# Two inner sums of the first Winograd tree on VectorE instead of GpSimd

## The chip, the core and the metric

The program runs on one core of a Trainium2 chip. The core has five instruction queues that matter here: TensorE (PE in the profile, with its weight loads as PEld), VectorE (DVE), ScalarE (ACT), GpSimd (POOL) and SyncE (SP), which issues most of the transfers. The metric is the device time of one execution in microseconds (us). All times below are in us unless marked ns.

## What is computed

With x of shape (1024, 512), 64 weight matrices W_e of 512 x 512, a linear layer and a bias, all in float32:

```
out_lin = x @ lin_w.T + lin_b
xv = jnp.einsum('bf,efm->bem', x, weight)
zp = jnp.einsum('bf,efm->bem', jnp.square(x), jnp.square(weight))
interaction = 0.5 * jnp.sum(jnp.square(xv) - zp, axis=1)
return out_lin + interaction
```

The second einsum needs no product per e: since it is summed over e, the kernel sums the squared weights over e first (`w2_sum`) and multiplies x squared with that once. The first one is the work: 64 products of 1024 x 512 by 512 x 512, squared and summed.

## The kernel before, in words

The model columns and the 64 values of e are laid out so that a *group* is one weight block of 512 features by 2048 columns. A group is multiplied by Winograd's form of Strassen's scheme, with seven products in place of eight, applied twice. At the outer level the weight block has four quarters, W11, W12, W21 and W22 (tiles `w11`, `w12`, `w21`, `w22a` or `w22b`), two sums `T1` and `T2`, and seven outer products, numbered 1 to 7; each is one call of `tree(s, g, i, order)`, with `RHS` naming the tile it reads. At the inner level a tree has again seven products, which I call p1 to p7, on the quarters b11, b12, b21, b22 of its tile and on four *inner sums*: t1 = b12 - b11, t2 = b22 - t1, t3 = b22 - b12, t4 = b21 - t2. p5 reads t1, p6 reads t2, p7 reads t3 and p4 reads t4; p1, p2 and p3 read quarters as they were loaded. The four sums go into four rings of two buffers each, `t1_0`, `t1_1` and so on; the first tree (`s` = 0) takes those with `_0`, the next one those with `_1`.

The X side (`x_all`, parts `X1` to `X7`, each with seven slots) is built once at the start from the quarters of x, by ACT copies and DVE sums, and stays in SBUF. In the same opening stretch the kernel computes the linear layer with four large products of its own (`lin_product`, line 461, the operands `oa`, `ob` and the DVE sums `w22b`) and, later and in between the first trees, a joint tree of three small products (`lin_tree`, line 821; its own inner sums are the POOL operations that write `ob`).

A tree's products go into three PSUM banks: `b3` takes p5 and then p3 on top of it, `b1` takes p1 and then p2, and a ring of two, `b2`, takes a copy of p1 on which p6, p7 and p4 are added one after another. Between them ACT copies banks to SBUF (`p5`, `p53`, `b2`), and DVE adds them (`oa1` after p6, `oa3` after p7). So the next product into a bank waits for the ACT copy or the DVE sum that reads it.

What runs where, and in which order on each queue, is settled by a planner in the file itself (`class Plan`). Every operation is added with its cost on the engines that may run it, its reads and its writes; PE's order is given by a key. `order()` works out the latest start of everything backwards from PE's sequence and then simulates the engines forward, each taking the ready operation with the earliest latest start. An operation added with `both=True` is one on DVE with two inputs in SBUF; for these the planner lengthens either DVE's or POOL's work when they overlap. The emitted queues are in order: an instruction that waits holds everything behind it.

Lines that the change and the prediction touch: `two_input` (306) makes a sum or difference for one engine, and line 312 is its instruction, whatever the engine; `tree` (646) with the loop over the four sums (650 to 657), `product` (663, matmuls at line 668) and the order of products at the end (726 to 743); `PLACE_0`, the order of the very first tree's products, p5, p1, p3, p6 first; `x_sum` (409), the X-side sums, recorded at 312 or 417; `outer_sum` (608), which for the first group makes `T1` and `T2` on DVE in halves.

Of the kernel before, what the change touches and what calls it, by code (L numbers as in the profile page):

```python
# [27 lines left out]
PE, DVE, ACT, POOL, SP = "PE", "DVE", "ACT", "POOL", "SP"  # L28
# [170 lines left out]
def kernel(  # L199
# [61 lines left out]
    buf = {}  # L261
# [39 lines left out]
    plan = Plan()  # L301
# [4 lines left out]
    def two_input(engine, o, a, b, sub, size=1024):  # L306

        costs = {DVE: 0.08 + 1.06 * size / 1024, POOL: 0.14 + 2.19 * size / 1024}

        def emit(e):  # L310
            f = engines[e].tensor_sub if sub else engines[e].tensor_add
            f(o, a, b)  # L312

        return {engine: costs[engine]}, emit

    def whole(o, a, b, psum=False):

        costs, emit = two_input(DVE if psum else POOL, buf[o], buf[a], buf[b], False)
        plan.add(costs, emit, (a, b), (o,))

    def act(o, i, func, reads, writes, cost=1.04):
        def emit(_):
            if func is None:
                nc.scalar.copy(o, i)  # L324
            elif func == "negative":
                nc.scalar.mul(o, i, -1.0)
            else:
                nc.scalar.activation(o, i, func)  # L328

        plan.add({ACT: cost}, emit, reads, writes)  # L330
# [262 lines left out]
    def w(g, q):  # L593
        return q + "ab"[g % 2] if q == "w22" else q
# [37 lines left out]
    def finish(g, i, n, pos):  # L632

        row, col = {2: (0, 0), 3: (0, 1), 4: (1, 0), 5: (1, 1)}[i]
        q, cc = divmod(pos, 2)
        b, m = (row * 2 + q) * G, (col * 2 + cc) * MI
        act(buf[n], buf[n], AF.Square, (n,), (n,), 1.07)
        reduce(buf[acc_name[g]][:, b:b + G, m:m + MI], buf[n], (n,), ((acc_name[g], i, pos),))
# [7 lines left out]
    def tree(s, g, i, order):  # L646
        r = w(g, RHS[i])
        b11, b21, b12, b22 = (buf[r][:, c, k, :] for c in range(NCB) for k in range(KH))
        t = {k: t_ring[k]() for k in range(1, 5)}
        for k, a, b, reads in (  # L650
            (1, b12, b11, (r,)),
            (2, b22, buf[t[1]], (r, t[1])),
            (3, b22, b12, (r,)),
            (4, b21, buf[t[2]], (r, t[2])),
        ):
            costs, emit = two_input(POOL, buf[t[k]], a, b, True, 512)
            plan.add(costs, emit, reads, (t[k],))
        rhs = {
            1: (b11, r), 2: (b21, r), 3: (b22, r), 4: (buf[t[4]], t[4]),
            5: (buf[t[1]], t[1]), 6: (buf[t[2]], t[2]), 7: (buf[t[3]], t[3]),  # L660
        }

        def product(p, b, first):
            op, name = rhs[p]

            def emit(_):
                for j in range(G):
                    nc.tensor.matmul(  # L668
                        buf[b][:, j, :], buf[f"X{i}"][:, SLOT[p], ts(j, P)], op,
                        start=first, stop=True, skip_group_check=True,  # L670
                    )

            plan.add({PE: PAIR}, emit, (name, f"{'Y' if p == 7 else 'X'}{i}", b), (b,),
                     key=7 * s + (PLACE if s else PLACE_0)[p])

        def copy(o, b):
            act(buf[o], buf[b], None, (b,), (o,))

        def target(pos):
            if i == 2 and order.index(2) < order.index(6):  # L680
                return c_ring()
            return f"{TARGET[i]}{pos}"

        def early(pos):

            return pos == 3 and i in ADDEND_FROM and (
                order.index(i) - order.index(ADDEND_FROM[i]) > 1
            )

        def outer_psum(b, pos):  # L690

            if i == 1:
                copy(f"oa{pos}", b)
            elif i == 5:
                o = c_ring()
                whole(o, f"oa{pos}", b, psum=True)
                whole(f"ob{pos}", f"ob{pos}", b, psum=True)
                finish(g, i, o, pos)
            else:
                o = target(pos)  # L700
                whole(o, b, f"{ADDEND[i]}{pos}", psum=True)
                if i in (2, 4, 3):
                    finish(g, i, o, pos)

        def outer_sbuf(b, p, pos):

            if i == 1:
                whole(f"oa{pos}", b, p, psum=True)
            elif i == 5:
                o = c_ring()  # L710
                whole(p, b, p, psum=True)
                whole(o, f"oa{pos}", p)
                whole(f"ob{pos}", f"ob{pos}", p)
                finish(g, i, o, pos)
            else:
                a, o = f"{ADDEND[i]}{pos}", target(pos)
                if early(pos):
                    whole(o, b, p, psum=True)
                else:
                    z = p if o == a else o  # L720
                    whole(z, b, p, psum=True)
                    whole(o, z, a)
                if i in (2, 4, 3):
                    finish(g, i, o, pos)

        b2, p5, p53 = b2_ring(), p5_ring(), p53_ring()
        product(5, "b3", True)
        if early(3):
            whole(p5, "b3", f"{ADDEND[i]}3", psum=True)
        else:  # L730
            copy(p5, "b3")
        product(3, "b3", False)
        copy(p53, "b3")
        product(1, "b1", True)
        copy(b2, "b1")
        product(6, b2, False)
        outer_sbuf(b2, p53, 1)
        product(2, "b1", False)
        outer_psum("b1", 0)
        product(7, b2, False)  # L740
        outer_sbuf(b2, p5, 3)
        product(4, b2, False)
        outer_psum(b2, 2)

    def turn(g, tiles, half=True):

        row = tuple((acc_name[g], i, pos) for i, pos in acc_parts if (i in (2, 3)) + 2 * (i in (4, 5)) & tiles)
        b = {1: slice(0, NB // 2), 2: slice(NB // 2, NB), 3: slice(0, NB)}[tiles]
        a, t = buf[acc_name[g]][:, b, :], buf["turned"][:, b, :]
        size = (b.stop - b.start) / NB  # L750
        names = tuple(("turned", h) for h in range(2) if tiles & 1 << h)
        if half:
            plan.add({ACT: 0.2 + 0.25 * size}, lambda _: nc.scalar.mul(a, a, 0.5), row, row)
        plan.add(
            {DVE: 0.1 + 0.27 * size},
            lambda _: nc.vector.transpose(
                t.rearrange("p n m -> p (n m)"), a.rearrange("p n m -> p (n m)")
            ),
            row, names,
        )  # L760
        return b, names
# [141 lines left out]
    def group(g, before={}):  # L903
        acc_name[g] = acc_ring()
        for q in range(4):
            load(g, q)
        outer_sum(g, 1)
        outer_sum(g, 2)
        w_squares(g, "w12")
        order = ORDER if g else ORDER_0  # L910
        for idx, i in enumerate(order):
            if i == 1:
                w_squares(g, "w11")
            if i == 2:
                w_squares(g, "w21")
            if i == 7:
                outer_sum(g, 3)
            if i == 4:
                outer_sum(g, 4)
            if i == (5 if g < NG - 1 else 2):  # L920
                w_squares(g, "w22")
            if idx == 1 and 0 < g < 8:
                x_squares((1, 2, 4, 5, 6, 7, 3)[g - 1])
            if idx in before:
                before[idx]()
            tree(7 * g + (g > 0) + idx + sum(idx >= b for b in before), g, i, order)

    for g in range(NG - 1):
        group(g, {} if g else {2: lin_tree})
        b, names = turn(g, 3)  # L930
# [237 lines left out]
    for h in (1, 0):  # L1168
        b, names = turn(last, 1 + h, h == 1)
# [57 lines left out]
```

## Time and profile before

| | us |
|---|---|
| three timed runs | 1402.46, 1402.54, 1408.55 (median 1402.54) |
| the profiled execution | 1407.72 |
| its span, first to last instruction | 1405.9 |
| PE busy | 1397.0 (99%) |
| DVE busy | 1092.5 (78%) |
| POOL busy | 1056.2 (75%) |
| ACT busy | 714.8 (51%) |
| mean granted TensorE clock | 0.998 |

A profile is one execution. Its lines name the engine, the program line and the operation as `out<-in` with the buffer numbers left out, so `t<-w` is an inner sum of a loaded quarter. In the timeline the first two columns are the start from the beginning of the span and the length; what stands in brackets is the idle time of that engine before the instruction and what ended it. A product of a tree is two matmuls of 128x512 in float32, and each shows as two records: four records are one product. The waits table gives total, number and longest wait. In the table of stretches each engine has its busy time and its count of instructions, and PEclk is the clock that TensorE was granted.

### The profile page before, as it was taken

Reading aid. Unit: us, or ns where it says so; the run is one execution under the profiler, and the core shown is the slowest. Engines: PE = TensorE matmul, PEld = TensorE weight load, DVE = VectorE, ACT = ScalarE, POOL = GpSimd, SP = SyncE. Lnnn points to the kernel's source line nnn. Section 1 sums busy time; section 2 is a strip of 40 time slices with the busy share of each in tenths; the row PEclk is TensorE's granted clock in tenths of the full one; section 3 lists DMA queues with packets and bytes.
Section 4 is the critical chain, followed back from the end, with each engine's and each line's share of the span. In section 5 each row is a group of like instructions: output and inputs, shape, how many; then the busy total and the mean of one; then the engine's idle time right before and its main releaser. Section 6 shows DMA issues by size and latency. Waiting matters only on the chain.

```text
span 1405.9 us, 10715 instructions
## 1 busy us (share of the span) xinstructions
PE 1397.0 (99%) x3314; PEld 631.8 (45%) x3314; DVE 1092.5 (78%) x985; ACT 714.8 (51%) x756; POOL 1056.2 (75%) x752
## 2 busy tenths in 40 slices
PE   8999999999999999999999999999999999999998
PEld 4544444444444444444444444444444444444454
DVE  4898696877969778596877959678696877959676
ACT  4546364554736456374544636455373544636444
POOL 5697786867778686786868778686786958678994
PEclk9999999999999999999999999999999999999999
DMA  7397473836739285482826638184572827538363
GB/s 269 75 205 195 119 199 86 222 111 162 216 116 217 97 195 183 120 213 77 236 65 170 162 90 214 37 195 131 123 180 77 228 57 178 155 96 207 101 164 113
DMA packets 55816, 212.90 MB, mean 151 GB/s; under 512 B 21521, under 2 KB 23057, under 8 KB 33873
## 3 DMA queue, kind: packets, MB, share of 16 engines
q0 software_dynamic: 13136, 84.81, 31.2%
q1 hardware_dynamic: 40352, 125.12, 25.5%
q10 hardware_dynamic: 2272, 2.30, 0.5%
q8 instruction: 27, 0.44, 0.1%
q14 instruction: 29, 0.23, 0.1%
HBM read 180.75 MB, written 14.02 MB: 139 GB/s over the span
## 4 chain that ended last, share of the span: by engine, by line
PE 98%; DMA 1%; DVE 0%; POOL 0%; SPq 0%; ACTq 0%; issue 0%; DVEq 0%
PE b L668 96%; PE b L821 1%; PE b L1140 1%; DMA w<-weight 1%; DMA ob<-lin_wT 0%; POOL t L312 0%; DVE x_all L312 0%; SPq L354 0%; DVE c L312 0%; ACTq L361 0%; DVE w_sum L335 0%; DVE T L1119 0%; DVEq L1223 0%; DVE T L1152 0%; DVE ob L860 0%
## 5 line engine op out<-in xcount | busy, mean ns | idle before, releaser
L668 PE MATMUL b<-t,x_all 128*128 128x512 f32 x1792 | 807.9, 594 | 3.4 <-POOL t L312 3.4
L668 PEld LDWEIGHTS b<-t,x_all 128*128 128x128 f32 x1792 | 341.4, 191 | 428.9 <-issue 418.7
L668 PE MATMUL b<-w,x_all 128*128 128x512 f32 x768 | 358.2, 593 | 0.0
L312 POOL TENSOR_TENSOR t<-w 128x512 f32<-128x512 f32 x128 | 174.5, 1364 | 145.6 <-PE b L668 77.1
L324 ACT COPY p<-b 128x1024 f32<-128x1024 f32 x165 | 165.5, 1003 | 183.2 <-PE b L668 178.4
L668 PEld LDWEIGHTS b<-w,x_all 128*128 128x128 f32 x768 | 146.3, 191 | 183.7 <-issue 182.7
L312 POOL TENSOR_TENSOR t<-w,t 128x512 f32<-128x512 f32 x128 | 171.7, 1342 | 56.9 <-PE b L668 56.8
L328 ACT ACTIVATE oa<-oa 128x1024 f32<-128x1024 f32 x124 | 129.6, 1057 | 148.0 <-DVE oa L312 148.0
L324 ACT COPY b<-b 128x1024 f32<-128x1024 f32 (+1 forms) x114 | 113.5, 996 | 136.0 <-PE b L668 132.4
L668 PE MATMUL b<-T,x_all 128*128 128x512 f32 x384 | 180.3, 593 | 0.0
L335 DVE TENSOR_REDUCE acc<-oa 128x16 f32<-128x1024 f32 x124 | 148.9, 1212 | 36.7 <-ACT oa L328 36.7
L312 DVE TENSOR_TENSOR oa<-b,p 128x1024 f32<-128x1024 f32 x95 | 115.8, 1219 | 49.1 <-PE b L668 49.1
L335 DVE TENSOR_REDUCE w_sum<-wsq 128x16 f32<-128x1024 f32 x128 | 153.8, 1209 | 0.2 <-ACT wsq L328 0.2
L328 ACT ACTIVATE c<-c 128x1024 f32<-128x1024 f32 x77 | 79.6, 1055 | 125.9 <-DVE c L312 84.3
L312 POOL TENSOR_TENSOR t<-T 128x512 f32<-128x512 f32 x64 | 87.3, 1364 | 52.3 <-issue 31.0
L668 PEld LDWEIGHTS b<-T,x_all 128*128 128x128 f32 x384 | 73.1, 190 | 90.8 <-issue 88.6
L312 DVE TENSOR_TENSOR p<-b,p 128x1024 f32<-128x1024 f32 x79 | 96.5, 1221 | 20.9 <-PE b L668 16.8
L312 DVE TENSOR_TENSOR ob<-b,p 128x1024 f32<-128x1024 f32 x48 | 58.7, 1222 | 64.8 <-PE b L668 64.7
L328 ACT ACTIVATE wsq<-w 128x1024 f32<-128x1024 f32 x96 | 98.1, 1053 | 5.6 <-DMA w<-weight 3.0
L312 POOL TENSOR_TENSOR t<-T,t 128x512 f32<-128x512 f32 x64 | 81.8, 1279 | 21.1 <-PE b L668 21.0
L312 POOL TENSOR_TENSOR c<-oa,p 128x1024 f32<-128x1024 f32 x32 | 84.7, 2648 | 0.0
L312 DVE TENSOR_TENSOR oa<-b,oa 128x1024 f32<-128x1024 f32 x62 | 75.7, 1220 | 9.5 <-PE b L668 9.5
(114 smaller groups left out, 1411.0 us busy)
## 6 DMA issues: line engine op xcount, KB each, us to landing
w<-weight SPq DMA_DIRECT2D x48, 1024.0 KB, 5.3
T<-weight POOLq DMA_DIRECT2D x45, 1024.0 KB, 8.9
T<-weight SPq DMA_DIRECT2D x30, 1024.0 KB, 7.3
w<-weight POOLq DMA_DIRECT2D x16, 1024.0 KB, 11.0
w<-T POOLq DMA_DIRECT2D x16, 1024.0 KB, 6.9
w22a<-weight SPq DMA_DIRECT2D x8, 1024.0 KB, 10.6
w22b<-weight SPq DMA_DIRECT2D x8, 1024.0 KB, 10.6
c<-xT SPq DMA_DIRECT2D x9, 512.0 KB, 6.2
```

Source lines behind the costliest of these rows:

```text
L312: f(o, a, b)
L324: nc.scalar.copy(o, i)
L328: nc.scalar.activation(o, i, func)
L335: lambda _: nc.vector.tensor_reduce(o, i.rearrange("p a (m e) -> p a m e", e=E), axis=AX.X, op=ALU.add),
L668: nc.tensor.matmul(buf[b][:, j, :], buf[f"X{i}"][:, SLOT[p], ts(j, P)], op, start=first, stop=True, skip_group_check=True,)
L821: nc.tensor.matmul(buf[b][:, u, lo:lo + Q], op[z], buf[f"X{x}"][:, SLOT[p], :], start=first and not lo, stop=True, skip_group_check=True,)
L1140: nc.tensor.matmul(o, ap[:, k, ts(u, P)], in_rows(o, buf[raw[i]][:, k, lo:hi]), start=first and k == 0, stop=k == 1, skip_group_check=True,)
```

## The change

In `tree`, the first two inner sums t1 and t2 of the tree with `s` = 0, which is the first tree of the first group and reads W11, are added for DVE instead of POOL, with `both=True`; t3 and t4 of that tree, and all four sums of every other tree, stay on POOL.

```diff
             (3, b22, b12, (r,)),
             (4, b21, buf[t[2]], (r, t[2])),
         ):
-            costs, emit = two_input(POOL, buf[t[k]], a, b, True, 512)
-            plan.add(costs, emit, reads, (t[k],))
+            engine = POOL if s or k > 2 else DVE
+            costs, emit = two_input(engine, buf[t[k]], a, b, True, 512)
+            plan.add(costs, emit, reads, (t[k],), both=engine == DVE)
```

The planner then emits other queues on two engines, in the opening stretch only. PE, ACT and SP keep their orders. DVE's queue, with the line numbers of the kernel before, changes from the fourteenth instruction on:

```
before                               after
x_all<-x_all,oa   (L417, for X6)     x_all<-x_all,oa   (L417, for X6)
x_all<-oa,oa      (X7)               t1
x_all<-x_all,oa   (L417, X3)         x_all<-x_all,oa   (L417, X3)
x_all 128x2x256                      t2
x_all 128x256                        x_all<-oa,oa      (X7)
x_all 128x2x256                      x_all 128x256
x_all 128x256                        oa1<-b2,p53       (after p6)
x_all 128x2x256                      x_all 128x2x256
oa1<-b2,p53       (after p6)         x_all 128x256
x_all 128x256                        x_all 128x2x256
T1, first half                       x_all 128x256
oa3<-b2,p5        (after p7)         x_all 128x2x256
                                     T1, first half
                                     oa3<-b2,p5        (after p7)
```

On POOL, with "next" for the sums of the second tree and `ob` for those of the linear joint tree:

```
before: t1, t3, t2, next t1, ob, ob, t4, next t2, next t3, next t4, ob x6, w12<-weight
after:  t3, ob, ob, next t1, next t3, next t2, t4, next t4, ob x6, w12<-weight
```

## The prediction

> **What bounds the kernel now.** I read the chain of waits first: 98% of the span is PE, and after the opening it is one unbroken piece of matmuls.
>
> ```profile
> 57 pieces in order of time: start us, us, what
> ...
> 8.92 7.38 DMA w<-weight
> 16.30 0.07 issue
> 16.38 5.68 POOL t L312
> 22.05 0.04 issue
> 22.10 17.18 PE b L668 x36
> ...
> 66.40 1292.65 PE b L668 x3012
> ```
>
> So the span is the opening, up to where the first tree's first product starts (22.10), and then PE's work. An edit can only help where PE waits, and the table of PE's waits has four entries:
>
> ```profile
> PE b L668 <- POOL t L312: 3.4, 1, 3.4
> PE b L387 <- PEq L1216: 0.8, 1, 0.8
> PE b L821 <- DVE c L860: 0.6, 1, 0.6
> PE b L461 <- DVE w22b L312: 0.2, 1, 0.2
> ```
>
> The largest is the wait of p5 for t1, the first of the two sums that the change moves. PE's timeline and the table of stretches show that it costs more than its length:
>
> ```profile
> 15.09 3.60 PE L461 MATMUL b<-x_all,w22b 128*128 128x512 f32 x8
> 22.10 3.44 PE L668 MATMUL b<-t,x_all 128*128 128x512 f32 x4 [3.41 <-POOL t L312]
> 25.38 3.60 PE L668 MATMUL b<-w,x_all 128*128 128x512 f32 x8
> ```
>
> ```profile
> 19.00:22.00 3.00, 0.00 (x0) 0.00 (x0) 1.92 (x5) 0.99 (x2) 3.00 (x1) 0.94 1.01 369
> 23.00:24.00 1.00, 1.00 (x3) 0.37 (x2) 0.00 (x0) 0.00 (x0) 1.00 (x2) 0.50 1.02 397
> 26.00:28.00 2.00, 2.00 (x6) 0.81 (x5) 0.00 (x0) 1.24 (x2) 2.00 (x4) 1.00 0.76 293
> ```
>
> PE has nothing from 18.69 (22.10 less 3.41) to 22.10, and then p5, four records, takes 3.44 where the next eight take some 3.43: the granted clock is 0.50 right after the gap and 1.00 later. Why t1 is late stands in the timelines of POOL and DVE:
>
> ```profile
> 16.38 5.67 POOL L312 TENSOR_TENSOR t<-w 128x512 f32<-128x512 f32 x1 [15.93 <-DMA w<-weight]
> 22.01 1.26 POOL L312 TENSOR_TENSOR t<-w 128x512 f32<-128x512 f32 x1
> ```
>
> ```profile
> 17.23 1.22 DVE L417 SCALAR_TENSOR_TENSOR x_all<-x_all,oa 128x1024 f32<-128x1024 f32 x1
> 18.36 2.56 DVE L312 TENSOR_TENSOR x_all<-x_all 128x512 f32<-128x512 f32 x5
> 30.80 1.23 DVE L312 TENSOR_TENSOR oa<-b,p 128x1024 f32<-128x1024 f32 x1 [9.88 <-PE b L668]
> ```
>
> The same 128x512 sum takes 1.26 once DVE is idle, and 5.67 while DVE runs X-side sums back to back until 20.92 (18.36 plus 2.56). POOL ends 1.13 after that, nearly one undisturbed sum later. I read it as POOL shut out until DVE stops.
>
> **What the change removes and adds.** Removed from POOL: t1 (5.67 as it stood) and t2 (1.26). Added to DVE: two sums of 128x512 with both inputs in SBUF. DVE does this size in 0.69 (its sums into w22b at 9.14 and 11.75), so 1.38 in all. t1 now comes directly behind the X6 sum, which ran from 14.96 to 16.18, and must wait for w11, seen by POOL at 16.38: done at 16.38 + 0.69 = 17.07. The trace shows no DVE sum and POOL sum released by one transfer, so I bound it. Below, DVE is not hindered: 17.07. Above, POOL's t3 goes first and DVE waits for one sum: 16.38 + 1.26 + 0.69 = 18.33. I take the lower, as the DVE rows at 17.23 and 18.36 kept their usual lengths with POOL waiting. Either way t1 is there before PE has finished the linear products at 18.69, so p5 follows them without a gap.
>
> The gain at that place: 3.41 of waiting, and 3.44 - 1.72 = 1.72 of half clock, for 1.72 is a product at full clock (half of 3.43). Sum 5.13.
>
> A rule speaks against counting the second term. The Trainium skill, page "TensorE: Matmul & The Clock Gate", section "Part 1: The HAM clock gate", says that the clock falls after an idle window of about 3.4 us which runs freely, whatever the kernel does; the gap here is about as long as that window, so it may or may not fall in another execution. By the rule the sum would be 3.4 in an execution where it doesn't fall, by the row 5.1.
>
> **Whether the next waits swallow it.** With p5 at 18.69, a product each 1.72: p1 20.41, p3 22.13, p6 23.85, the next tree's p5 25.57, and everything behind 5.13 earlier than now. One by one:
>
> - p1 needs bank b1, read by ACT until 18.73 + 1.26 = 19.99. Cover 0.4. ACT's copies follow PE as they do now.
> - p6 needs t2: t1 at 17.07, the X3 sum 1.22, t2 0.69, so 18.98. Cover 4.9; with a POOL sum ahead of each still 2.4.
> - The next tree's p5 needs its t1 from POOL, now behind t3 and two `ob` sums. DVE's run ends at 18.98 + 1.22 (X7) + 0.42 = 20.62; POOL's t3 1.13 later, 21.75; the `ob` sums 0.72 and 0.45, and the sum 1.26: 24.2. Cover 1.4. If the 5.67 was a slow first instruction and not DVE, t3 ends at 22.05 and the sum at 24.5. Cover 1.1.
> - In order, DVE now holds five X sums behind oa1, which waits for p6 (25.57). They ran before, in the 9.88 of idle time. New: oa1 25.7 to 26.9, the five (0.69 three times, 0.42 twice) 2.91, T1's half 1.22, so 31.1. Who waits: oa3, due at 37.59 - 5.13 = 32.46, and PE's first joint product, which needs X3, X6 and X7, at 39.11 - 5.13 = 33.98. Cover 1.4. From below nothing is lost. From above, POOL is at work just then and each DVE sum can meet one: t4 and the next t4 (1.27 each), then `ob` of 0.72, 0.45, 0.72 and so on, in sum some 4.7. Then DVE is 4.7 - 1.4 = 3.3 late, p4 loses about 1.7 of it (oa3 done at 32.46 + 3.3 + 1.23 = 37.0, p4 due at 40.41 - 5.13 = 35.28), and at most 3.3 is lost by 60.11, where PE already waits 0.62 for DVE. The nearest row is DVE's stay at 16.09 to 20.92, where its queue never paused for a waiting POOL; I take nothing lost.
> - Behind POOL's `ob` sums stands its transfer onto w12 (issued at 40.58 after a wait of 4.41): two sums fewer are ahead of it, and its releaser moves with PE. The loads on SP from 58.04 on wait for buffers that PE frees; they move along. The loads before that are issued by 20.96, as now.
>
> On the port, the skill's page "SBUF — State Buffer", section "Who interferes with whom", says that a DVE instruction with two SBUF inputs and a GpSimd instruction that reads SBUF exclude each other, the first one holding for its whole instruction. By the rule the added sums lengthen POOL's exclusion by 1.38 and could be shut out themselves for one POOL sum; the row shows four DVE instructions on end past a waiting POOL, which is more than one instruction's hold. Both leave p5 at 18.69, so the sum is 5.1 by either.
>
> **Sum.** Span 1405.9 - 5.1 = 1400.8; profiled execution 1407.7 - 5.1 = 1402.6. That execution lies 5.2 above the median of the runs, 1402.54, and near the slowest, 1408.55. I subtract from the median: 1402.5 - 5.1 = **1397.4**.
>
> **The rivals.**
>
> 1. *The timed runs don't have the whole stall.* The 5.2 between profile and median is just the size of the stall; if the two runs at 1402.5 had POOL through between DVE's sums, nothing is left to win: 1402.5. If only their clock did not fall, 1402.5 - 3.4 = 1399.1. Against it: DVE shows no pause from 9.14 to 20.92, so a transfer that lands a little sooner or later doesn't let POOL in; the three runs give no trace. Chance 0.22.
> 2. *The wait moves to DVE's late X sums* (fourth point): 1.7 to 3.3 given back, 1399.1 to 1400.7. For it: DVE's sum of T1 at 32.61 took 1.47 and an X sum 0.75 beside POOL. Against: 9.9 idle on DVE. Chance 0.13.
> 3. *More than the stall goes.* If the half clock lasts twice as long in the timed runs (1.7 more) and the 0.62 before the joint product goes too: 5.1 + 2.3 = 7.4, so 1395.1. The profile shows one stretch of 3.44 only. Chance 0.12.
> 4. *Slower.* POOL's t3 and DVE's t1 are released by the same landing. If POOL takes the port at 16.38 and holds it through a slow first instruction of 5.67, t1 runs from 22.05 to 22.74, and p5 starts at 22.8 in place of 22.10, again after a gap and at half clock: 0.7 slower, 1403.2. It decides as soon as t1 ends after 22.05. Against: in the row of 5.67 DVE worked on unhindered, so that instruction held nothing. Chance 0.05.
>
> **How the numbers follow.** The forecast has 0.48. The range is 1395.0 to 1403.0: it holds the forecast, rivals 1 and 2 and the end of rival 3, and leaves out rival 4 and the scatter that the run at 1408.55 shows. Half a per cent, about what a measurement of this kernel can tell from no change, is 7.0: faster means below 1395.5, slower above 1409.6. The forecast itself lies inside. Faster: rival 3 (0.12) and 0.02 of scatter below the forecast, 0.14. Slower: rival 4 met by a median that falls on the upper run, 0.03. The same: 0.83. The likeliest case alone, with its scatter: 1396.5 to 1398.5.
>
> **What would show it.** Right: t1 on DVE at about 16.4 and 0.69 long; no entry "PE b <- t" in PE's waits; the first tree's p5 at 18.7 and 1.72 long, with a clock of 1.00 from 19 to 26; the joint tree's first product at 34.0; a span of 1400.8. Wrong: t1 of over 2 us (rival 4); PE waiting for DVE between 33 and 37 (rival 2); a span 5 shorter with times that stay at 1402.5 (rival 1).

## The result, and the profile after

The changed kernel takes 1403.28 us, the median of 22 runs (1402.35 to 1403.90). In the same sessions 22 runs of the kernel before gave a median of 1408.27. The ratio is 0.9978, with a 95% interval of 0.9968 to 0.9989; the means, 1403.24 and 1406.30, have the same ratio. So the kernel is some 3.1 us faster, 0.2%, which the interval tells from nothing but which lies within the half per cent of the forecast's "same". The forecast was 1397.4 with a range of 1395.0 to 1403.0. The time lies above it.

The medians differ by 5.0 and the means by 3.1 because the runs of before fall into two groups, and those after into one:

| 22 runs each | below 1405 | 1408 and more |
|---|---|---|
| before | 10 (1402.46 to 1404.19) | 12 (1408.13 to 1410.71) |
| after | 22 (1402.35 to 1403.90) | 0 |

The profile of before (1407.72) lies just under the upper group, and I count it there. The median of three that I subtracted from, 1402.54, was a run of the lower one.

The profiled execution after took 1403.63 with a span of 1401.8, against 1405.9 before. PE's waits, total, number, longest:

```profile
PE b L461 <- DMA oa<-xT: 1.3, 1, 1.3
PE b L387 <- PEq L1217: 0.8, 1, 0.8
PE b L822 <- DVE c L861: 0.6, 1, 0.6
```

The wait of 3.4 for t1 is gone. A wait of 1.3 for a transfer of x has come in, at the first linear product; the change doesn't touch what lies ahead of it. It cost less than its length: in PE's timeline the last linear products start 1.02 later (16.11 against 15.09), and p5 follows the linear products at once:

```profile
7.42 5.42 PE L461 MATMUL b<-oa,ob 128*128 128x256 f32 x24 [1.30 <-DMA oa<-xT]
...
16.11 3.60 PE L461 MATMUL b<-x_all,w22b 128*128 128x512 f32 x8
19.54 1.88 PE L669 MATMUL b<-t,x_all 128*128 128x512 f32 x4
21.26 3.60 PE L669 MATMUL b<-w,x_all 128*128 128x512 f32 x8
```

p5 to p1 is 21.26 - 19.54 = 1.72, full speed. The table of stretches gives a clock of 1.00 there (third number from the end):

```profile
19.00:22.00 3.00, 3.00 (x8) 1.33 (x7) 3.00 (x3) 1.81 (x3) 3.00 (x4) 1.00 1.02 415
```

DVE and POOL tell the most. Their timelines, start, length, operation:

```profile
17.63 0.69 DVE L312 TENSOR_TENSOR t<-w 128x512 f32<-128x512 f32 x1 [0.55 <-DMA w<-weight]
18.24 2.29 DVE L417 SCALAR_TENSOR_TENSOR x_all<-x_all,oa 128x1024 f32<-128x1024 f32 x1
20.45 1.21 DVE L312 TENSOR_TENSOR t<-w,t 128x512 f32<-128x512 f32 x1
...
27.82 5.07 DVE L312 TENSOR_TENSOR x_all<-x_all 128x512 f32<-128x512 f32 x5
32.81 1.74 DVE L312 TENSOR_TENSOR T<-w,w 128x1024 f32<-128x1024 f32 x1
34.47 1.21 DVE L312 TENSOR_TENSOR oa<-b,p 128x1024 f32<-128x1024 f32 x1
```

```profile
17.68 1.77 POOL L312 TENSOR_TENSOR t<-w 128x512 f32<-128x512 f32 x1 [17.23 <-DMA w<-weight]
19.41 1.71 POOL L312 TENSOR_TENSOR ob<-w22b 128x256 f32<-128x256 f32 x1
21.08 0.90 POOL L312 TENSOR_TENSOR ob<-ob 128x128 f32<-128x128 f32 x1
```

I read this as the two engines taking turns, one instruction each. The X3 sum, 1.22 before, takes 2.29 and ends 1.08 after POOL's t3 (17.68 + 1.77 = 19.45), about one undisturbed sum later; the `ob` sum behind t3, 0.72 before, takes 1.71 and ends 0.59 after the X3 sum (20.53). In the profile of before DVE's sums kept their 1.22 and POOL's t1 took 5.67. So the first question for the experiments was why POOL is shut out in one execution and has its turn in another.

### The profile page after: what moved, and what is told of

Same layout as the page of the kernel before. It is cut to its first block, busy times and chain, and to the rows that moved or that the text cites. A ratio compares the mean times of both kernels' runs of the same rounds, so it can differ in the third digit from the quotient of the medians.

```text
span 1401.8 us, 10713 instructions
## 1 busy us (share of the span) xinstructions
PE 1395.2 (100%) x3314; PEld 630.1 (45%) x3314; DVE 1099.0 (78%) x987; ACT 715.0 (51%) x756; POOL 1054.8 (75%) x750
## 4 chain that ended last, share of the span: by engine, by line
PE 99%; DVE 0%; DMA 0%; SPq 0%; issue 0%; DVEq 0%
PE b L669 96%; PE b L822 1%; PE b L461 1%; PE b L1141 1%; DMA oa<-xT 0%; DVE x_all L312 0%; DVE c L312 0%; DVE w_sum L335 0%; SPq L354 0%; DVE T L1120 0%; DVEq L1224 0%; DVE T L1153 0%; DVE ob L861 0%; DVE c L861 0%; DVE w22b L861 0%
## 5 line engine op out<-in xcount | busy, mean ns | idle before, releaser
L312 POOL TENSOR_TENSOR t<-w 128x512 f32<-128x512 f32 x127 | 170.9, 1346 | 146.7 <-PE b L669 77.0
```

## The experiments

Each kernel is an edit of the kernel before unless another is named. Times are medians of 11 or 12 runs; the runs of before beside them are on the same chip. "Upper" and "lower" are the two groups of times of before.

**The kernel before, again.** No edit.

> The kernel before, unchanged, to see a second execution of it in the profile and the spread of its times. The 22 timed runs of before fall into two groups, 1402.5 to 1404.2 and 1408.1 to 1410.7; those of the changed kernel into one, 1402.4 to 1403.9. Theory A (POOL's t1 is shut out by DVE's sums in some executions and let through in others): both groups again, and a profile of the lower group has t1 ending before 19.5, a gap of PE under 1 and no half clock, one of the upper group has t1 near 5.7 long. Theory B (the stall is in every execution and the groups come from elsewhere): t1 near 5.7 long whatever the time of the run.

Measured: 1403.37 (1402.74 to 1404.51, and one of 1409.61); before, 35 runs: 24 below 1405, three from 1405.4 to 1406.7, eight from 1407.9 to 1409.4. This time the profile shows an execution of the lower group (1403.16). Its POOL and DVE timelines:

```profile
16.90 2.03 POOL L312 TENSOR_TENSOR t<-w 128x512 f32<-128x512 f32 x1 [16.45 <-DMA w<-weight]
```

```profile
13.98 1.23 DVE L312 TENSOR_TENSOR x_all<-oa,oa 128x1024 f32<-128x1024 f32 x1 [0.19 <-DMA oa<-xT]
...
16.59 1.22 DVE L312 TENSOR_TENSOR x_all<-oa,oa 128x1024 f32<-128x1024 f32 x1
17.73 2.29 DVE L417 SCALAR_TENSOR_TENSOR x_all<-x_all,oa 128x1024 f32<-128x1024 f32 x1
```

t1 ends at 18.93, 1.12 after the X7 sum, the X3 sum gives way, and PE's waits have no entry for t1. p5 follows the linear products (15.62 and two products of 1.72) at once:

```profile
19.05 1.92 PE L668 MATMUL b<-t,x_all 128*128 128x512 f32 x4
```

So theory A holds for this execution of the lower group: the same program, and no stall. The mean clock points the same way: 0.999 or 1.0 in every run below 1405, 0.997 to 0.999 in the eight upper ones, lower as a stretch of half clock would make it.

**Only t1 moved.**

```diff
-            engine = POOL if s or k > 2 else DVE
+            engine = DVE if s == 0 and k == 1 else POOL
```

(against the changed kernel)

> Only t1 on VectorE, t2 back on GpSimd. If p5's wait for t1 is all that the change mends: one group of times at 1402.4 to 1403.9 as with both sums moved, no wait of PE for t1. If t2 was the other half of it: PE waits for t2 before p6, by up to 1.5 us, and the times lie above 1404.

Measured: 1402.35 (1401.74 to 1403.18), ratio to before 0.9987 (0.9977 to 0.9996). In its profile PE waits neither for t1 nor for t2. Moving t2 adds nothing.

**DVE held until POOL has made four sums.** `first` are t1, t3, t2 and the next tree's t1, `mark["t"]` is the last of these, `R7` the X7 sum.

```diff
+    first = [z for z in seq if z[1] == POOL and z[0].emit][:4]
+    seq = [z for z in seq if z not in first]
+    at = next(n for n, z in enumerate(seq) if z[0] is mark["R7"])
+    hold = SimpleNamespace(
+        emit=lambda _: nc.vector.tensor_copy(scratch[:, 0:1], mark["t"][:, 0:1])
+    )
+    seq[at:at] = first + [(hold, DVE)]
```

> Both sums stay on GpSimd; VectorE gets one copy of a single column that reads the next tree's t1, ahead of the X7 sum, so that its X sums start only when GpSimd has made t1, t3, t2 and the next t1. If the stall is exclusion by VectorE's run of sums: t1 takes 1.26, ends near 17.7, no gap of PE, times 1402.4 to 1404. If t1's 5.67 was a slow first instruction of GpSimd: t1 still takes over 5, the gap stays and the times keep two groups or lie at 1408 and above.

Measured: 1406.86 (1405.35 to 1407.53), no gain, and not the 1402.4 to 1404 that I expected. The cause of the stall is answered all the same: with DVE idle t1 takes its usual time.

```profile
17.12 1.27 POOL L313 TENSOR_TENSOR t<-w 128x512 f32<-128x512 f32 x1 [16.68 <-DMA w<-weight]
```

But the X sums, now from 22.17 on, meet POOL one by one, and a new wait takes the old one's place:

```profile
25.15 7.38 DVE L313 TENSOR_TENSOR x_all<-x_all 128x512 f32<-128x512 f32 x5
32.45 1.21 DVE L313 TENSOR_TENSOR oa<-b,p 128x1024 f32<-128x1024 f32 x1
```

```profile
33.71 3.56 PE L674 MATMUL b<-t,x_all 128*128 128x512 f32 x4 [2.23 <-DVE oa L313]
```

Five sums that took 2.56 undisturbed take 7.38, oa1 is late, and p7 waits 2.23 and then runs at half clock (3.56 for four records). This is rival 2 of the prediction, brought on by force: 4.8 lost on DVE (7.38 - 2.56), 4.0 on PE (2.23 of waiting, and 1.8 of half clock, as p7 and the product behind it took 5.24 from 33.71 on in place of 3.43).

**Three more matmuls in the gap.**

```diff
+        if op is last_lin:
+            for _ in range(3):
+                nc.tensor.matmul(
+                    buf["b3"][:, 0, :], zero[:, 0:P], zero, start=True, stop=True,
+                    skip_group_check=True,
+                )
```

> The kernel before with three further TensorE matmuls of zeros (128x512, into the bank that p5 then overwrites) between the linear products and p5, which fill some 2.6 us of the gap. If the half clock after the gap costs 1.7 us: the upper group falls from 1408 to 1410 to about 1407, p5 takes 1.72, and the wait for t1 remains with under 1 us visible; the lower group, if it has no gap, rises by up to 2.6 us. If the half clock costs nothing of its own: upper group as before.

Measured: 1406.24 (1404.69 to 1409.29). The profiled execution had no stall, and p5 started 2.6 late behind the zeros. By the expectation runs with the stall and runs without it come to nearly the same time here, and only one was profiled, so the price of the half clock could not be read; it was run again below.

**Only the order on DVE.** t1 and t2 stay on POOL, the five X sums go behind oa1.

```diff
+    late, oa1 = dve[at + 1:at + 6], dve[at + 6]      # at: the X3 sum
+    seq = [z for z in seq if z not in late]
+    seq[seq.index(oa1) + 1:seq.index(oa1) + 1] = late
```

> Both sums stay on GpSimd; only VectorE's order changes: the five X sums that follow the X3 sum go behind oa1, as the change puts them. VectorE's run then ends some 2.5 us sooner. Theory A (in the upper group GpSimd is shut out until VectorE's run ends): t1 ends about 2.5 us sooner in such executions, PE's gap shrinks from 3.4 to about 1, and the upper group comes down from 1408 to about 1404 to 1405. Theory C (in the upper group GpSimd's first sum is slow by itself, and its end 1.1 us after VectorE's run is chance): the upper group stays at 1408 and more, as often as in the kernel before.

Measured: 1404.65 (1403.28 to 1405.10), where 22 of the 35 runs of before lay at 1406.37 and more. The profile shows t1 shut out, but until DVE's shorter run ends:

```profile
17.23 1.22 DVE L417 SCALAR_TENSOR_TENSOR x_all<-x_all,oa 128x1024 f32<-128x1024 f32 x1
26.85 1.23 DVE L312 TENSOR_TENSOR oa<-b,p 128x1024 f32<-128x1024 f32 x1 [8.40 <-PE b L670]
```

```profile
19.62 1.98 PE L670 MATMUL b<-t,x_all 128*128 128x512 f32 x4 [0.93 <-POOL t L312]
```

DVE stops at 18.45; p5 starts at 19.62, 1.17 later, as it was 22.10 after 20.92 (1.18) in the profile of before. The gap shrinks from 3.41 to 0.93. That is theory A, with its numbers, and theory C is out: no run lies above 1405.10. The profile is of the fastest run, 1403.28; why seven others lie at 1404.55 to 1405.10 I have not traced.

**POOL's first sum earlier.**

```diff
+    nc.gpsimd.tensor_sub(buf["t4_1"], zero, zero)
```

> The kernel before with one further 128x512 difference on GpSimd at the very start, of zeros, into the next tree's t4, which is written again later. Theory A (shut out): nothing changes, two groups as in the kernel before, 1402 to 1404 and 1408 to 1410. Theory C (the first sum of GpSimd is slow by itself): the upper group is gone, all times at 1402 to 1404.5.

Measured: seven runs from 1402.51 to 1404.41, five from 1407.42 to 1410.25. Both groups stay, and the profile was of the upper one: t1 from 16.87 with DVE undisturbed until 20.91, and p5 at 22.08, again 1.17 after DVE's end. So a slow first sum on POOL is not the cause.

**Both kernels on one chip.** The changed kernel, and the one with only t1 moved.

> The changed kernel, on the same chip as the next one. Theory: one group of times, 1402 to 1404, equal to the lower group of the kernel before within 0.1%; no run above 1406.

> Only t1 on VectorE, once more, beside the changed kernel. If it is the better one: a median about 1 us below the changed kernel's, no run above 1404. If the earlier 1402.35 was the chip or the session: equal to the changed kernel within 0.3 us.

Measured: 1403.11 (1402.51 to 1403.75) with both moved, 1401.98 (1401.49 to 1402.82, and one of 1404.24) with only t1; ratios to before 0.9980 (0.9967 to 0.9993) and 0.9980 (0.9968 to 0.9992). The ratios don't separate the two kernels, the runs do: the means are 1403.16 and 1402.21, and eight of the eleven runs with t1 alone lie below all with both. So t1 alone is the better version, 1.1 below the changed kernel in the medians and 1.2 below the lower group of before. Some 0.6 of the 1.1 can be shown. With both moved PE waits 0.6 for the joint tree's DVE sum into `c`, behind an X sum that POOL holds up:

```profile
52.69 2.75 DVE L312 TENSOR_TENSOR x_all<-x_all 128x512 f32<-128x512 f32 x1
55.37 0.41 DVE L861 TENSOR_TENSOR c<-b,p 128x256 f32<-128x256 f32 x1
```

With t1 alone the planner puts the two the other way round, and the wait is not there:

```profile
52.65 0.41 DVE L861 TENSOR_TENSOR c<-b,p 128x256 f32<-128x256 f32 x1
52.98 1.61 DVE L312 TENSOR_TENSOR x_all<-x_all 128x512 f32<-128x512 f32 x1
```

From p5 to the end both profiles with t1 alone take 1381.4 (span less p5's start), and both with both sums moved 1382.2 and 1382.3, so some 0.8 of the difference lies behind p5. The rest I have not traced; p5's start varies by as much as 1.2 among these four profiles (18.54 to 19.69), with when x lands.

**What decides between turns and exclusion.** Two executions with turns (the kernel before, again, and the one with more matmuls) had a short pause on DVE before, of 0.19 and 0.22, waiting for x; the three with exclusion had none from 9.1 on. Two kernels make a pause by one small copy on DVE, in the second behind two copies on ScalarE, and leave both sums and all orders as before:

```diff
+        if op is mark["R7"]:      # first kernel: ahead of the X7 sum
+            nc.vector.tensor_copy(scratch[:, 0:1], buf["w11"][:, 0, 0, 0:1])
```

```diff
+        if op is mark["R5"]:      # second kernel: ahead of the X5 sum
...
+            nc.scalar.copy(buf["wsq_0"][:, 0, :], buf["X1"][:, 0:2, :].rearrange("p s b -> p (s b)"))
+            nc.vector.tensor_copy(scratch[:, 0:1], buf["wsq_0"][:, 0, 0:1])
```

> Both sums stay on GpSimd, orders as before; VectorE gets one copy of a single column of w11 ahead of the X7 sum, so that its run pauses until w11 has landed, the moment at which t1 starts on GpSimd. Theory D (GpSimd is shut out only where VectorE's run has no pause behind it; after a pause the two take turns): t1 ends within 3 us of its start in every execution, PE's gap is under 1, one group of times, 1402 to 1405. Theory E (which of the two happens is chance in every execution): two groups as in the kernel before.

> Both sums on GpSimd, orders as before; ahead of the X5 sum (13.48 in the profile of before) VectorE waits for two further copies on ScalarE into a buffer not used until later, a pause of some 0.4 us more than 2 us before w11 lands. Two executions whose profile shows the two engines taking turns had a pause of 0.2 at that place, those with t1 shut out had none. Theory D: no upper group, times 1402 to 1405. Theory E: both groups, 1402 to 1405 and 1408 to 1410.

Measured: 1403.01 (1401.95 to 1404.11) and 1403.45 (1402.80 to 1404.01), ratios 0.9981 (0.9970 to 0.9993) and 0.9986 (0.9976 to 0.9997). None of the 23 runs lies above 1404.2, and 12 of the 29 of before beside them lie at 1405.9 and more. In the first t1 takes 1.27 from 17.46 on. In the second the pause is over nearly 3 us before POOL starts at 17.27:

```profile
14.38 0.15 DVE L1200 COPY scratch<-wsq 128x1 f32<-128x1 f32 x1 [0.33 <-ACT wsq L1199]
...
17.17 1.22 DVE L313 TENSOR_TENSOR x_all<-oa,oa 128x1024 f32<-128x1024 f32 x1
18.30 2.28 DVE L418 SCALAR_TENSOR_TENSOR x_all<-x_all,oa 128x1024 f32<-128x1024 f32 x1
```

So theory D holds for what it says of times, and theory E is out: one copy of a column does what moving two sums does. How a pause of 0.33 acts on what happens 3 us later stays open. The moment at which POOL starts does not decide it: it is 0.10 after the start of the X7 sum both here (17.27 and 17.17, turns) and with the order alone (16.19 and 16.09, exclusion), and 0.31 and 0.29 after it in the two profiles of the kernel before, with turns and with exclusion.

**The matmuls of zeros, again.**

> The three further matmuls of zeros once more, as the first time nearly all executions were of the lower group. In executions with the stall they fill 2.6 us of the gap of 3.4 and keep the clock up: 1.7 to 2.8 below the upper group of the kernel before, so 1405.5 to 1407; in those without, 2.6 above the lower group, 1405 to 1406.5. So the two groups should meet, and few runs lie at 1408 or above. If the half clock costs nothing by itself, the upper group stays at 1408 to 1410.

Measured: 1406.68 (1405.50 to 1407.19); six of the 29 runs of before lie at 1408.3 and more. The groups meet, as they would if the half clock had a price of its own, but with six in 29 a dozen runs may lack the upper group by chance, and one of the first dozen lay at 1409.29. The experiment doesn't show the price; it is read from the profiles.

## Why the prediction was wrong, point by point

- *The gain at that place, 5.13:* right for the executions that have the stall. The two medians differ by 4.99. In the profile t1 is 0.69 long, p5 comes without a gap, takes 1.72, and the clock is 1.00. The second profile with t1 alone has its last linear products at 15.10, where before had 15.09, so it can be set beside it:

```profile
15.10 3.60 PE L461 MATMUL b<-x_all,w22b 128*128 128x512 f32 x8
18.54 1.88 PE L669 MATMUL b<-t,x_all 128*128 128x512 f32 x4
20.25 3.60 PE L669 MATMUL b<-w,x_all 128*128 128x512 f32 x8
```

p1 starts at 20.25 and not at 25.38, 5.1 earlier. The two terms of the sum were each off by some 0.15, in opposite ways, which is luck: p5 came 22.10 - 18.54 = 3.56 late, and not 3.41, and the half clock cost 25.38 - 22.10 - 1.72 = 1.56, and not 1.72, for the 3.44 is the length of four records, which at full clock is 1.88. The profile of the upper group from the earlier-first-sum kernel shows the second term to be a range: there p5, p1 and p3 took 7.98 (22.08 to 30.06) in place of 5.15, so 2.8 was lost. Thirteen of the 99 runs of before beside the experiments lie between the groups, at 1405.4 to 1407.3; the wait without the half clock would give about 1403.2 + 3.6 = 1406.8, but no profile shows one, and what they have stays open.
- *The base, "I subtract from the median: 1402.5 - 5.1":* this is the step that failed. Two of the three runs, 1402.46 and 1402.54, lie in the lower group, whose profile (1403.16) shows no stall, so by all signs they had no 5.1 to lose; they have no trace of their own. The sum made against the profiled execution was 1402.6, and against its span 1400.8; measured are 1403.28, and spans of 1400.6 to 1402.1, 1401.8 in the profile. Without the 1.02 by which its linear products came later, that is 1400.8. Against the lower group of before (13 runs, median 1403.18, beside the 1403.11 of the changed kernel on that chip) nothing is gained, as rival 1 said: 1402.5. It had 0.22.
- *Against rival 1, "DVE shows no pause from 9.14 to 20.92, so a transfer that lands a little sooner or later doesn't let POOL in":* true of the profiled execution and false of others. The transfers of x do land later in some, DVE then pauses by 0.19, and POOL has its turn. I saw that 5.2 between profile and median was the size of the stall and gave it less than half the forecast's chance.
- *Exclusion, "POOL shut out until DVE stops":* right for the executions without a pause on DVE (before, order alone, first sum earlier), where POOL's end moved with DVE's. Not always: with a pause the engines take turns. The row showed more than the "four DVE instructions on end": from 16.38 on there are seven, the X7 sum (already running), the X3 sum and five more, until 20.92.
- *DVE's late X sums, 2.91:* mis-sized. They took 5.07 beside a busy POOL, and oa3 came at 34.47, about 1.0 after p7 let it go. The bound of 4.7 more held. PE didn't feel it: p4 started at 36.28, oa3 ended at 35.68. In the kernel with DVE held the same five took 7.38 and PE waited.
- *The next tree's t1 on POOL, bank b1, t2:* no wait there, as forecast.
- *Rival 3* (more than the stall): no run below 1402.35, though a half clock of twice the length does occur (last section). *Rival 4* (t1 late behind POOL): t1 and t3 were released together, and t1 went first, 0.69 long.

Of the Trainium skill's page "SBUF — State Buffer", section "Who interferes with whom": turns are what its rule of one holder for one instruction would give, here 2.29 for 1.22. The exclusion over seven instructions (4.5 us, 16.38 to 20.92) goes beyond it. Of the Trainium skill's page "TensorE: Matmul & The Clock Gate", section "Part 1: The HAM clock gate": a gap of 3.41 cost the clock, as its window of 3.4 would allow, but so did one of 2.23 in the kernel with DVE held; the measurement decides. Gaps of 0.93 and 1.48 did not.

## What to carry to other kernels

Before subtracting a stall that a profile shows from a median, ask whether the runs behind the median have it: compare the profiled execution's own time with each of them, and if the distance is the size of the stall, the forecast has two ends, not one. Where GpSimd makes something urgent beside a long run of two-input VectorE sums, look at more than one execution: here a pause of 0.2 to 0.3 us, up to 3 us earlier, went with its being let in and not shut out. Moving the one urgent sum to VectorE took that chance away, and it was enough to move that one. VectorE work put off into GpSimd's busy time cost nearly double here (5.07 for 2.56), so its new place needs slack for that.

## What the runs showed of the hardware that was not expected

- Two ways of sharing between VectorE and GpSimd in one program: GpSimd's 128x512 sum took 5.67 beside an unbroken run of VectorE sums with both inputs in SBUF, all at their usual length, and 2.03 with turns, where VectorE's 1.22 became 2.29. In every profile of a kernel with t1 on GpSimd, turns went with a pause on VectorE up to 3 us earlier, the shortest of 0.19, and forcing a pause left no run above 1404.2 among 23.
- The half clock came after a gap of 2.23 and not after gaps of 0.93 and 1.48. After two gaps of 3.4 it cost 1.6 in the profile of before and 2.8 in that of the kernel with the earlier first sum, which is part of the spread of the upper group. The granted clock (third number from the end) in stretches of 1 us shows when it fell and when it came back. The profile of before, the kernel with the earlier first sum, and the one with DVE held:

```profile
21.00:22.00 1.00, 0.00 (x0) 0.00 (x0) 0.00 (x0) 0.00 (x0) 1.00 (x1) 0.83 0.93 354
25.00:26.00 1.00, 1.00 (x4) 0.52 (x3) 0.00 (x0) 0.42 (x1) 1.00 (x2) 0.96 1.05 406
```

```profile
20.00:21.00 1.00, 0.00 (x0) 0.00 (x0) 0.91 (x2) 0.00 (x0) 1.00 (x1) 0.89 0.97 377
27.00:28.00 1.00, 1.00 (x3) 0.39 (x2) 0.00 (x0) 0.00 (x0) 1.00 (x2) 0.70 0.44 170
```

```profile
33.00:34.00 1.00, 0.29 (x1) 0.29 (x2) 1.00 (x2) 0.00 (x0) 1.00 (x2) 0.99 0.00 0
37.00:38.00 1.00, 1.00 (x3) 0.53 (x2) 0.69 (x1) 0.00 (x0) 0.00 (x0) 0.80 0.00 0
```

All stretches between show 0.50. Taking the clock as either 1 or a half, 0.83 means that it fell 0.34 before 22.00, and so on: it was at a half from 21.7 to 25.1, from 20.8 to 27.6 and from 34.0 to 37.4. That is an estimate of 3.4, 6.8 and 3.4, once and twice the same length. What lay in PE's gap cost nothing, so 3.0 of the first and 5.5 of the second were paid, at half each: 1.5 and 2.8. In the third the clock fell 0.3 after PE had started again (33.71).
